# Four graph-attention layers on one core: earlier mask gathers, and two jobs of layer 2 moved to other engines

## The chip, the core and the metric

The kernel runs on one core of one Trainium2 chip. A core has a matmul engine (TensorE), three engines for elementwise work (VectorE, ScalarE, GpSimd), and a queue that issues direct transfers (SyncE). They run side by side and meet at semaphores. The metric is the device time of one execution in microseconds (us). Lower is better.

## The reference

The input is a matrix `x` of 4096 nodes by 256 features and a 0/1 adjacency of 4096 by 4096, which is sparse for most nodes: its density falls with the node's number. Four attention layers follow one another. Each normalizes the rows, applies a relu, projects, and lets every target node average its neighbours with softmax weights; the result is added to `x`.

```python
h = jnp.maximum(_layernorm(x), 0.0)
h = h @ W                                  # layer 2: four heads of 64 columns
e = leaky_relu((h @ a1)[:, None] + (h @ a2)[None, :], 0.2)
attention = softmax(where(adj > 0, e, -inf), axis=1)
x = x + f(attention @ h)                   # f: identity in layers 0 and 2, elu in layer 1
```

Layer 3 has a positive and a negative attention, projects their results together and ends in an elu. Layers 0 and 1 have one head, layer 2 has four, layer 3 counts as two.

## The kernel before, in words

**Tiles and lists.** The 4096 nodes are 32 tiles of 128; four tiles are a block, so there are eight blocks. Targets in the first blocks (`DENSE = (4, 2, 1, 1)` of them in layers 0 to 3) are computed densely: all 32 source tiles are multiplied against the whole block of 512 targets. Later target tiles are computed from a list: four fixed source tiles (`DP`), whose masks are in `mpre`, and then `CAPS[T]` more steps, each of which takes 128 source rows picked by an index. `CAPS` falls from 12 in tile 4 to 6 in tile 31.

**The lists.** `list_sources` works out in layer 0, block by block, which sources a tile needs. Its last step writes `idx_T`, a table of row numbers with one column for each step. Lists for blocks 4 to 7 come up in layer 0 between dense blocks, since those targets are listed there already; those of blocks 1, 2 and 3 follow as the dense blocks' masks are read.

**The gathers.** A listed step needs two indirect DMAs, both issued by GpSimd. `s_gg` (L1189) fetches 128 rows of the layer's table of projected nodes, once for each layer. `mlist` (L895) fetches the mask columns that belong to them; it is fetched once, kept on chip, and used by all later layers. There are 715 of the first kind and 218 of the second. `masks_of` is the queue of mask gathers still to be issued. `gather_masks(n)` issues up to `n` of them after a step of the plan, in the queue's order; `gather_masks(CAPS[T], T)` fetches what tile `T` still lacks at the moment it is needed. The queue's order before is blocks 4 to 7, then 2 and 3, then 1.

**A step of the plan.** `run` walks through a hand-made plan of steps. Each step passes four stages: fetch (gathers are issued), begin (ScalarE, layer 2 only), weigh (VectorE) and multiply (TensorE), at leads of 0, 2, 3 and 6 steps (`LEAD`). After each multiplied step it advances a clock by the unit's `cost` and works off three queues at the unit's `rates`: `posts` (ends of tiles and rows for the next layer), `lists_q`, and the mask gathers. GpSimd executes in exactly the order in which its instructions are written; the order on the other engines is decided by a scheduler.

**Weights in layer 2.** A weight is max(grow, g) times the mask. VectorE does this with one pass for a head (L999). For `nact` of the four heads ScalarE begins instead: relu(grow * g - 1) (L985), and one VectorE pass over these heads together adds 1 and multiplies by the mask (L1008). `nact` is 2 before.

**The end of a tile in layer 2.** `end2` is a generator in `posts`. ScalarE copies the accumulator to `o`, TensorE transposes it, VectorE divides by the sums into `y` and adds `y` to `x` (L1132). A `yield t` lets the plan's clock go on by `t` before the next part is written. `node_rows` of layer 3 starts on a pair of tiles when both are marked in `stored`; its first instruction is the statistics of `x` on VectorE (L672), and its last stores the projected rows to the table. No listed step of a layer can gather before all rows of its table are stored.

**Order of tiles.** In layer 2 the plan begins with 36 dense steps. Tiles 8 to 31 follow and then 4 to 7. The rest of the dense steps is spread between the first 14 tiles. Layer 1 begins with 16 dense steps and has 48 more, two after each listed tile.

Of the kernel before, what the change touches and what calls it, by code (L numbers as in the profile page):

```python
# [20 lines left out]
NT = N // P  # L21
IB = 512
NIB = N // IB
IT = IB // P
# [429 lines left out]
DP = CH  # L454
JT = NT - DP
TS0 = IT
DENSE = (4, 2, 1, 1)
# [3 lines left out]
CAPS = (25, 17, 15, 13, 12, 11, 11, 10, 10, 9, 9, 9, 8, 8, 8, 8) + (8,) + (7,) * 7 + (6,) * 8  # L461
# [11 lines left out]
def list_layers(ctx: ExitStack, tc: tile.TileContext, a: dict, out: bass.AP, flag):  # L473

    nc = tc.nc
# [31 lines left out]
    x = keep.tile([P, NT, D], F32, name="x")  # L507
# [134 lines left out]
    def pump(queue, n, width=1, force=False):  # L642

        k = 0
        while n and k < min(width, len(queue)):
            if queue[k][1] > clock[0] and not force:
                k += 1
                continue
            n -= 1
            try:  # L650
                queue[k][1] = clock[0] + (next(queue[k][0]) or 0.0)
            except StopIteration:
                queue.pop(k)

    def ensure(done):
        while not done():
            assert posts
            pump(posts, 1, force=True)
# [139 lines left out]
    def list_sources(ib, seen, pool, consts):  # L798
# [81 lines left out]
    index = {}  # L880

    masks_of = [
        (T, k)
        for b0, b1 in ((DENSE[0], NIB), (DENSE[1], DENSE[0]), (1, DENSE[1]))
        for T in range(b0 * IT, b1 * IT)
        for k in range(CAPS[T])
    ]
# [1 line left out]
    def gather_masks(n, tile=None):  # L889

        for T, k in list(masks_of):
            if not n or tile is None and T not in index:
                break
            if tile in (None, T):
                nc.gpsimd.indirect_dma_start(  # L895
                    out=mlist[:, OFFS[T] + k, :],
                    out_offset=None,
                    in_=mask_t[T // IT],
                    in_offset=bass.IndirectOffsetOnAxis(ap=index[T][:, k : k + 1], axis=0),
                    element_offset=T % IT * P,  # L900
                )
                masks_of.remove((T, k))
                n -= 1
# [207 lines left out]
    def end2(u, it, T):  # L1111
        big = layers[2].big
        o = big.tile([DH + 1, HEADS, P], F32, name=f"s_o_{T}", tag="o", bufs=2)
        if u.nt == 1:
            nc.scalar.copy(o, u.accs[0])
        else:
            for h in range(HEADS):
                nc.scalar.copy(o[:, h, :], u.accs[h][:, it * P : (it + 1) * P])
        yield 1.0
        tp = ps_mm.tile([P, HEADS, DH + 1], F32, name=f"s_oT_{T}", tag="mm")  # L1120
        for h in range(HEADS):
            nc.tensor.transpose(
                tp[:, h, :], o[:, h, :], ident[0 : DH + 1, 0 : DH + 1]
            )
        yield 3.0
        rz = small.tile([P, HEADS], F32, name=f"s_rz_2_{T}", tag="rz4")
        nc.vector.reciprocal(rz, tp[:, :, DH])
        y = big.tile([P, HEADS, DH], F32, name=f"s_y2_{T}", tag="y2", bufs=2)
        nc.vector.tensor_tensor(
            y, tp[:, :, 0:DH], rz.unsqueeze(2).to_broadcast([P, HEADS, DH]), op=ALU.mult  # L1130
        )
        nc.vector.tensor_add(x[:, T, :], x[:, T, :], y.rearrange("p h o -> p (h o)"))  # L1132
        stored[T] = 2

    firsts = {}
# [39 lines left out]
    def listed_sources(L, T, pool):  # L1175
        heads = list(range(L.H))

        def get(i):
            if i < DP:
                g = L.g[:, i, :] if L.l == 0 else L.pre[:, i, :]  # L1180
                m = mpre[:, i, T * P : (T + 1) * P]
            else:
                ensure(lambda: all(L.ready))
                while T not in index:
                    pump(lists_q, 1, force=True)
                gather_masks(CAPS[T], T)
                k = i - DP
                g = pool.tile([P, GW[L.l]], F32, name=f"s_gg_{L.l}_{T}_{k}", tag="gg")
                nc.gpsimd.indirect_dma_start(  # L1189
                    out=g,  # L1190
                    out_offset=None,
                    in_=L.table,
                    in_offset=bass.IndirectOffsetOnAxis(ap=index[T][:, k : k + 1], axis=0),
                )
                m = mlist[:, OFFS[T] + k, :]
            return heads, [g[:, h * L.part : (h + 1) * L.part] for h in heads], m

        return get

    with ExitStack() as phase:  # L1200
# [28 lines left out]
        L0 = weights(0, prep, prep, nc.scalar)  # L1229
# [80 lines left out]
        def block(ib):  # L1310
            masks = {}

            def get(jt):
                if jt % CH == 0:
                    masks[jt // CH] = mask_chunk(ib, jt // CH)
                for k, at in enumerate(sides):
                    if at == ib * NT + jt:
                        mask_chunk(DENSE[0] + k // NCH, k % NCH)
                ensure(lambda: L0.ready[jt])
                return [0], [L0.g[:, jt, :]], masks[jt // CH][:, jt % CH, :]  # L1320

            return Unit(L0, ib * IT, IT, NT, get, big="growb", rates=(2, 2, 1))

        load_x(0)
        load()
# [9 lines left out]
        for ib in range(DENSE[0]):  # L1335
            for step in block(ib).plan():
                plan.append(step)
                if ib * NT + step[1] >= LISTED0:
                    n = 1 + step[1] % 2
# [10 lines left out]
    gat = ctx.enter_context(tc.tile_pool(name="s_gather", bufs=9))  # L1350
    stream = ctx.enter_context(tc.tile_pool(name="s_stream", bufs=3))
    for l in (2, 3):
        L = weights(l, late, late, nc.sync)
# [11 lines left out]
    for l in (1, 2, 3):  # L1365
        L = layers[l]

        def all_sources(L, T0, nt, heads, per):


            held = {}
            n = L.part
            cols = slice(heads[0] * n, (heads[-1] + 1) * n)
            w = slice(T0 * P, (T0 + nt) * P)

            def get(i):
                jt, k = divmod(i, per)
                jt = ORDER[L.l][jt // CH] * CH + jt % CH
                mine = heads[k : k + 1] if per > 1 else heads
                if jt < DP:  # L1380
                    ensure(lambda: L.ready[jt])
                    return mine, [L.pre[:, jt, h * n : (h + 1) * n] for h in mine], mpre[:, jt, w]
                if jt % CH == 0 and k == 0:
                    ensure(lambda: all(L.ready[jt : jt + CH]))
                    gt = stream.tile(
                        [P, CH, n * len(heads)], F32, name=f"s_gs_{L.l}_{T0}_{jt}_{heads[0]}", tag="gs"
                    )
                    nc.sync.dma_start(gt, table_rows(L.table, jt)[:, :, cols])
                    mt = stream.tile([P, CH, nt * P], U8, name=f"s_ms_{L.l}_{T0}_{jt}_{heads[0]}", tag="ms")
                    nc.sync.dma_start(mt, table_rows(mask_t[T0 // IT], jt)[:, :, 0 : nt * P])  # L1390
                    held["t"] = gt, mt
                gt, mt = held["t"]
                h0 = heads[0]
                return (
                    mine,
                    [gt[:, jt % CH, (h - h0) * n : (h - h0 + 1) * n] for h in mine],
                    mt[:, jt % CH, :],
                )

            return get  # L1400


        if l == 3:
            one = Unit(L, 0, IT, NT, all_sources(L, 0, IT, [0], 1), big="growb", heads=[0])
            two = Unit(L, 0, IT, NT, all_sources(L, 0, IT, [1], 1), big="growb", heads=[1], like=one)
            first = one.plan() + two.plan()
        else:
            per = L.H
            first = []
            for ib in range(DENSE[l]):  # L1410
                first += Unit(
                    L,
                    ib * IT,
                    IT,
                    NT * per,
                    all_sources(L, ib * IT, IT, list(range(L.H)), per),
                    big="o" if ib else "growb",
                    cost=0.9 if l == 2 else 1.7,
                    per=per,
                    rates=(2, 0, 1),  # L1420
                ).plan()
        tiles = []
        tail = DENSE[0] if l == 1 else DENSE[1]
        for T in (*range(tail * IT, NT), *range(DENSE[l] * IT, tail * IT)):
            u = Unit(
                L, T, 1, DP + CAPS[T], listed_sources(L, T, gat), cost=(0, 0.9, 1.2, 0.9)[l], nact=(0, 0, 2, 0)[l]
            )
            tiles.append(u.plan())


        alone, over_tiles = ((0, 0), (16, 24), (36, 14), (16, 28))[l]
        plan += first[:alone]
        rest = first[alone:]
        for k, t in enumerate(tiles):
            plan += t
            n1, n2 = (len(rest) * min(j, over_tiles) // over_tiles for j in (k, k + 1))
            plan += rest[n1:n2]
# [60 lines left out]
```

## Time and profile before

| | before |
|---|---|
| time, median of 3 runs | 1764.71 us (1761.51 to 1771.69) |
| span of the profiled run | 1771.9 us |
| TensorE busy | 1670.8 us (94%), 9268 instructions |
| VectorE busy | 1331.1 us (75%) |
| GpSimd busy | 1068.4 us (60%), 1043 instructions |
| ScalarE busy | 610.2 us (34%) |
| table gathers, L1189 | 715, 1042 ns on the mean |
| mask gathers, L895 | 218, 1105 ns on the mean |
| last table gather of layer 0 issued | 509.7 us |
| last attention matmul of layer 1 ends | 847.0 us |
| first attention matmul of layer 3 | 1352.8 us |

The shares are means over four layers with different limits, so they don't tell what a stage waits for. In the profile's rows PE is TensorE, PEld its weight loads, DVE VectorE, ACT ScalarE, POOL GpSimd and SP SyncE. A row of a group ends with the idle time of its engine before these instructions and with what ended it. Issue time of a DMA isn't counted as busy.

### The profile page before, as it was taken

Reading aid. Unit: us, or ns where it says so; the run is one execution under the profiler, and the core shown is the slowest. Engines: PE = TensorE matmul, PEld = TensorE weight load, DVE = VectorE, ACT = ScalarE, POOL = GpSimd, SP = SyncE. Lnnn points to the kernel's source line nnn. Section 1 sums busy time; section 2 is a strip of 40 time slices with the busy share of each in tenths; the row PEclk is TensorE's granted clock in tenths of the full one; section 3 lists DMA queues with packets and bytes.
Section 4 is the critical chain, followed back from the end, with each engine's and each line's share of the span. In section 5 each row is a group of like instructions: output and inputs, shape, how many; then the busy total and the mean of one; then the engine's idle time right before and its main releaser. Section 6 shows DMA issues by size and latency. Waiting matters only on the chain.

```text
span 1771.9 us, 29224 instructions
## 1 busy us (share of the span) xinstructions
PE 1670.8 (94%) x9268; PEld 1386.0 (78%) x9268; DVE 1331.1 (75%) x3908; ACT 610.2 (34%) x1802; POOL 1068.4 (60%) x1043
## 2 busy tenths in 40 slices
PE   6989999989999899897989999999999999999997
PEld 4877777768878778675467887889998888888886
DVE  6778898878764676654869988998886577777765
ACT  5531011011030132111357767699984011111101
POOL 9665655736566777777775444455571655555563
PEclk9998798989989999998999999999999999999999
DMA  8889767935264444443233333233332666656554
GB/s 270 275 268 296 221 208 230 333 103 184 53 167 138 119 130 136 119 130 88 66 75 97 85 104 86 80 105 104 91 101 74 206 201 181 181 168 183 168 171 125
DMA packets 134530, 271.08 MB, mean 153 GB/s; under 512 B 23186, under 2 KB 52288, under 8 KB 134368
## 3 DMA queue, kind: packets, MB, share of 16 engines
q0 software_dynamic: 48272, 127.55, 27.3%
q1 hardware_dynamic: 85260, 141.04, 24.0%
q8 instruction: 77, 1.26, 0.3%
q14 instruction: 85, 0.70, 0.1%
q10 hardware_dynamic: 836, 0.53, 0.1%
HBM read 228.91 MB, written 40.12 MB: 152 GB/s over the span
## 4 chain that ended last, share of the span: by engine, by line
PE 72%; DVE 10%; DMA 9%; POOL 4%; issue 3%; ACT 2%; SPq 0%; DVEq 0%; ACTq 0%; POOLq 0%
PE s_acc L1035 43%; PE s_accm L1060 17%; PE s_pj L727 6%; DMA s_gg<-table,idx 5%; DVE s_p L999 3%; DMA s_raw<-in_adjT 3%; PE idx_ps L866 2%; POOL mlist L895 2%; PE s_sT L933 1%; PE s_tp L695 1%; DVE first L857 1%; DVE s_m L1277 1%; POOL s_gg L1189 1%; ACT s_p L985 1%; DVE s_p L1008 1%
## 5 line engine op out<-in xcount | busy, mean ns | idle before, releaser
L1189 POOL DMA_INDIRECT s_gg<-table,idx x715 | 745.0, 1042 | 581.8 <-PE s_acc L1035 239.1
L999 DVE SCALAR_TENSOR_TENSOR s_p<-s_grow,s_gg,mlist 128x128 f32<-128x128 f32 x1151 | 367.8, 346 | 195.3 <-DMA s_gg<-table,idx 124.6
L1035 PE MATMUL s_acc<-s_gg,s_p 128*128 128x257 f32 x1430 | 358.1, 391 | 28.0 <-DVE s_p L999 27.7
L1035 PEld LDWEIGHTS s_acc<-s_gg,s_p 128*128 128x128 f32 x1430 | 267.5, 193 | 84.0 <-DVE s_p L999 48.4
L1035 PE MATMUL s_acc<-g,s_p 128*128 128x257 f32 x1152 | 298.3, 404 | 5.0 <-DVE s_p L999 5.0
L895 POOL DMA_INDIRECT mlist<-mask_t,idx x218 | 240.9, 1105 | 76.0 <-issue 56.4
L1035 PEld LDWEIGHTS s_acc<-g,s_p 128*128 128x128 f32 x1152 | 226.4, 202 | 38.2 <-DVE s_p L999 6.7
L999 DVE SCALAR_TENSOR_TENSOR s_p<-s_grow,pre,mpre 128x128 f32<-128x128 f32 (+1 forms) x576 | 190.3, 369 | 39.7 <-PE s_acc L1035 31.2
L1035 PE MATMUL s_acc<-s_gs,s_p 128*128 128x257 f32 x896 | 217.1, 398 | 0.0
L1060 PE MATMUL s_accm<-s_p,s_gg 128*65 128x128 f32 x1744 | 207.2, 274 | 3.4 <-DVE s_p L1008 2.7
L1035 PEld LDWEIGHTS s_acc<-s_gs,s_p 128*128 128x128 f32 x896 | 178.0, 200 | 32.0 <-DVE s_p L999 4.9
L1060 PEld LDWEIGHTS s_accm<-s_p,s_gg 128*65 128x65 f32 x1744 | 193.9, 138 | 8.6 <-DVE s_p L1008 5.1
L985 ACT ACTIVATE s_p<-s_grow,s_minus,s_gg 128x128 f32<-128x128 f32 x436 | 186.7, 486 | 36.8 <-DMA s_gg<-table,idx 23.1
L999 DVE SCALAR_TENSOR_TENSOR s_p<-s_grow,s_gs,s_ms 128x512 f32<-128x512 f32 x224 | 162.4, 749 | 45.0 <-PE s_accm L1060 21.0
L1035 PE MATMUL s_acc<-pre,s_p 128*128 128x257 f32 x768 | 181.8, 381 | 0.3 <-ACT s_y L1146 0.2
L727 PE MATMUL s_pj<-s_w,s_hT 128*128 128x259 f32 (+3 forms) x640 | 165.4, 399 | 7.7 <-ACT s_hT L697 3.7
L939 ACT ACTIVATE s_grow<-s_sT 128x256 f32<-128x256 f32 (+2 forms) x136 | 46.8, 367 | 341.8 <-PE s_sT L933 332.8
L1035 PEld LDWEIGHTS s_acc<-pre,s_p 128*128 128x128 f32 x768 | 143.4, 191 | 21.8 <-ACT s_y L1146 0.6
L727 PEld LDWEIGHTS s_pj<-s_w,s_hT 128*128 128x128 f32 x640 | 121.8, 197 | 31.5 <-ACT s_hT L697 6.4
L1060 PE MATMUL s_accm<-s_p,pre 128*65 128x128 f32 (+1 forms) x928 | 120.3, 284 | 4.8 <-DVE s_p L1008 4.8
L1060 PEld LDWEIGHTS s_accm<-s_p,pre 128*65 128x65 f32 x928 | 103.9, 138 | 21.6 <-issue 14.6
L985 ACT ACTIVATE s_p<-s_grow,s_minus,pre 128x128 f32<-128x128 f32 x224 | 96.3, 487 | 19.1 <-issue 11.9
(123 smaller groups left out, 1658.1 us busy)
## 6 DMA issues: line engine op xcount, KB each, us to landing
s_raw<-in_adjT SPq DMA_DIRECT2D x128, 512.0 KB
s_gs<-table SPq DMA_DIRECT2D x28, 516.0 KB
mask_t<-s_m SPq DMA_DIRECT2D x56, 256.0 KB
s_gg<-table,idx POOLq DMA_INDIRECT x715, 3.5
s_ms<-mask_t SPq DMA_DIRECT2D x35, 256.0 KB
table<-s_g SPq DMA_DIRECT2D x28, 258.0 KB
table<-g SPq DMA_DIRECT2D x8, 516.0 KB
x<-in_x SPq DMA_DIRECT2D x8, 512.0 KB
```

Of the source, the lines that this page charges most:

```text
L695: nc.tensor.transpose(tp[:, c, :], zs[k][:, c * P : (c + 1) * P], ident)
L727: nc.tensor.matmul(ps, lhsT=hT[:, c, :], rhs=L.w[:, c, k * (D + 6) : k * (D + 6) + cols], start=(c == 0), stop=(c == 1),)
L857: nc.vector.tensor_tensor(first, place, lof[:, t, j : j + half].unsqueeze(1).to_broadcast([P, P, half]), op=ALU.is_equal,)
L866: nc.tensor.matmul(ps[:, 0:cap], lhsT=first[:, :, j % half], rhs=val[:, 0:cap, j * IT + t], start=(j == 0), stop=(j == JT - 1),)
L895: nc.gpsimd.indirect_dma_start(out=mlist[:, OFFS[T] + k, :], out_offset=None, in_=mask_t[T // IT], in_offset=bass.IndirectOffsetOnAxis(ap= ...
L933: nc.tensor.transpose(ps[:, h - h0, it, :], L.s[:, T0 + it, h : h + 1].to_broadcast([P, P]), ident)
L939: nc.scalar.activation(grow[:, h1:h2, :], ps[:, h1 - h0 : h2 - h0].rearrange("p h a b -> p h (a b)"), AF.Exp, scale=scale,)
L985: nc.scalar.activation(w[:, h, :], u.grow[:, h, :], AF.Relu, scale=g[h][:, n - 1 : n], bias=minus)
L999: nc.vector.scalar_tensor_tensor(p[:, k, :], u.grow[:, h, :], g[k][:, n - 1 : n], m, op0=ALU.min if L.l == 3 and h == 1 else ALU.max, op1= ...
L1035: nc.tensor.matmul(u.accs[it][h], lhsT=p[:, k, it * P : (it + 1) * P], rhs=g[k][:, 0:n], start=first, stop=last,)
L1060: nc.tensor.matmul(u.regions[h], lhsT=g[k][:, 0 : DH + 1], rhs=p[:, k, :],  start=first and (u.nt > 1 or h == 0), stop=last, skip_group_ch ...
L1189: nc.gpsimd.indirect_dma_start(out=g, out_offset=None, in_=L.table, in_offset=bass.IndirectOffsetOnAxis(ap=index[T][:, k : k + 1], axis=0),)
```

## The change

Three parts. First, the queue of mask gathers takes blocks 1, 2 and 3 in their own order after blocks 4 to 7; an entry whose list isn't ready is passed over where it stopped the walk before; dense steps of layer 0 issue two mask gathers in place of one, and the dense steps of layer 2 issue none. It is for having the masks in before layers 1 and 2 need GpSimd for table gathers. Second, the addition to `x` at the end of a tile in layer 2 goes from VectorE to GpSimd, 2.0 on the plan's clock after `y`. Third, in tiles 6, 9, ..., 30 of layer 2 ScalarE begins three heads and VectorE does one by itself. Parts two and three are for relieving VectorE.

```diff
-        for b0, b1 in ((DENSE[0], NIB), (DENSE[1], DENSE[0]), (1, DENSE[1]))
+        for b0, b1 in ((DENSE[0], NIB), (1, DENSE[0]))
...
         for T, k in list(masks_of):
-            if not n or tile is None and T not in index:
-                break
-            if tile in (None, T):
+            if n and T in index and tile in (None, T):
                 nc.gpsimd.indirect_dma_start(
...
-        nc.vector.tensor_add(x[:, T, :], x[:, T, :], y.rearrange("p h o -> p (h o)"))
+        yield 2.0
+        nc.gpsimd.tensor_add(x[:, T, :], x[:, T, :], y.rearrange("p h o -> p (h o)"))
         stored[T] = 2
...
-            return Unit(L0, ib * IT, IT, NT, get, big="growb", rates=(2, 2, 1))
+            return Unit(L0, ib * IT, IT, NT, get, big="growb", rates=(2, 2, 2))
...
-                    rates=(2, 0, 1),
+                    rates=(2, 0, 1 if l == 1 else 0),
...
-                L, T, 1, DP + CAPS[T], listed_sources(L, T, gat), cost=(0, 0.9, 1.2, 0.9)[l], nact=(0, 0, 2, 0)[l]
+                L, T, 1, DP + CAPS[T], listed_sources(L, T, gat), cost=(0, 0.9, 1.2, 0.9)[l], nact=(0, 0, 3 if T % 3 == 0 else 2, 0)[l]
```

## The prediction

> **What bounds the kernel now.** I read the page's slices first, then the table of windows with boundaries at the layers' first and last matmuls, then GpSimd's timeline, then the chain. The slices say that TensorE is busy nearly everywhere, but a busy TensorE is modelled, so I looked for stretches where it waits.
>
> ```profile
> PE   6989999989999899897989999999999999999997
> POOL 9665655736566777777775444455571655555563
> PEclk9998798989989999998999999999999999999999
> ```
>
> The windows (PE, PEld, DVE, ACT, POOL busy with counts, then clock and DMA):
>
> ```profile
> 138.00:511.00 373.00, 349.41 (x1983) 292.08 (x1984) 305.06 (x781) 52.45 (x192) 218.79 (x193) 0.89 0.63 197
> 557.00:846.00 289.00, 261.27 (x1101) 205.59 (x1101) 174.18 (x544) 61.40 (x213) 220.83 (x224) 0.93 0.44 120
> 947.00:1157.00 210.00, 210.00 (x1409) 161.60 (x1407) 186.83 (x556) 145.67 (x373) 98.81 (x89) 1.00 0.33 88
> 1157.00:1353.00 196.00, 191.46 (x1610) 183.18 (x1609) 170.90 (x613) 177.36 (x498) 105.97 (x98) 1.00 0.35 97
> ```
>
> The reader is to see layer 1 (557 to 846): GpSimd is busy 221 of 289 us, which looks loose. Its timeline tightens it, because every gather is followed by 0.30 us of issue:
>
> ```profile
> 837.02 0.95 POOL L895 DMA_INDIRECT mlist<-mask_t,idx  x1 [0.30 <-issue]
> 838.28 0.94 POOL L895 DMA_INDIRECT mlist<-mask_t,idx  x1 [0.30 <-issue]
> ...
> 889.39 0.94 POOL L1189 DMA_INDIRECT s_gg<-table,idx  x1 [0.30 <-DMA mlist<-mask_t,idx]
> ```
>
> 224 x 0.30 = 67 us more, 288 of 289: GpSimd is full, and layer 1 is bound by its gathers. The lines from 837 to 889 are 36 mask gathers in a row at the turn to layer 2, ahead of layer 2's first table gather. The chain agrees (window 815 to 945):
>
> ```profile
> by line: POOL mlist L895 28.4%; DMA s_gg<-table,idx 14.8%; issue 12.6%; PE s_accm L1060 11.1%; DVE s_p L999 7.5%; DMA mlist<-mask_t,idx 5.8%; POOL s_gg L1189 5.1%; PE s_acc L1035 4.3%; DVE s_p L1008 3.0%; ACT s_p L985 2.9%; PE s_pj L727 0.7
> ```
>
> In layer 0 the chain runs over TensorE, loads of the adjacency and VectorE; GpSimd idles 95 us there (gaps over 0.31 us, 145 to 511, summed from the timeline). In layer 2 from 947 to 1157 the chain is TensorE alone; from 1157 to 1353 TensorE, VectorE and ScalarE are all near full. Layer 3 is TensorE's.
>
> **What the Trainium skill says.** "GPSIMD Engine Reference", Elementwise side-by-side cycle accounting: a two-input add takes about twice as long on GpSimd. The trace agrees: 128x256 adds take 861 ns on GpSimd (L685), 421 on VectorE (L1132). The same page, Key points: GpSimd shares SBUF interfaces with VectorE. The trace fits: a gather takes 0.94 us at least, but 218.79/193 = 1.13 on the mean in layer 0, 0.99 in layer 1 where VectorE is less busy. "TensorE: Matmul & The Clock Gate", What's actually happening: a window of little work halves TensorE's clock. The trace agrees: 0.66 in 890 to 900, after a wait. "DMA: Bandwidth & Descriptors", Anatomy of one DMA: about 2 us of fixed latency per gather; here a table gather lands 2.7 to 7.2 us after issue (median 3.5).
>
> **Part 1, mask gathers.** 218 remain; they move. From the order of GpSimd's instructions in both programs: before, layer 0 holds 105 mask and 105 table gathers; after, blocks 1 and 2 and 5 gathers of tile 12 join them, 44 + 37 + 5 = 86. Between layer 0's and layer 1's table gathers stand 14 masks in both. Layer 1's own stretch then has 174 table and 13 mask gathers, none from tile 23 on. The 36 at the turn and those inside layer 2's first tiles are gone.
>
> *Layer 0.* GpSimd works in order, and a mask gather waits for its tile's list. The lists come from VectorE, whose order here is unchanged: tile 20's is written at 189.2. After the change the gathers for tile 20 stand right behind tile 16's eight table gathers, so GpSimd waits there until 189.3 and has 296 - 29 - 8 = 259 gathers to go. At layer 0's pace (1.13 + 0.30 = 1.43) that is 370 us: the last is issued near 560, against 510 before. Behind these masks in the queue stand the table gathers of tiles 17 to 31; their multiplies (TensorE, then VectorE's weights) wait. I compared issue plus 4.5 us with the time of each multiply before: up to tile 20 they arrive within about 5 us, tile 22's are 16 late, tile 28's about 40. So layer 0 ends about 49 us later. At 1.25 (the uncontended pace) it would be 2, at 1.50 (more contention) 68; I take 1.43, since VectorE has the same work to do beside it.
>
> *Layer 1.* First table gather 22 us after layer 0's last, as before (509.7 to 531.9; the 14 masks take 18): 582. Then 187 x (0.99 + 0.30) = 240, plus 6 for the wait for buffers at the start (6.4 at 554): last gather 828. Before, the last matmul came 10 us after the last gather: 838. TensorE alone (each f32 matmul leaves two records; spacings from the chain): between 557 and 846 there are 901 attention records, so 450 matmuls, at 0.434 (64 records in 13.89 us) = 195, projections 23, transposes and rows 10: 228 us; 557 + 49 + 228 = 834. The two nearly meet. Layer 1 ends near 838 against 847: -9.
>
> *Turn to layer 2.* From 885 to 947 TensorE spends 62 us on 144 listed matmuls at 0.218 (24 records in 2.62 us), 13.5 dense ones at 0.86 (20 records in 8.75 us) and 5.4 us of projections and transposes, 48 us in all; the rest is waiting behind the masks, partly at half clock. With the queue free when the table is ready I count 10 of the 14 us: -10.
>
> **Part 2, the add on GpSimd.** Removed: 32 x 0.42 = 13.5 us of VectorE. Added: 32 x (0.86 + 0.30) = 37 us of GpSimd, and a wait: GpSimd's add waits for y, and behind it stand the next table gathers. Laying y's times in before against the gathers that follow each add in the new order, tiles 9 to 21 stop GpSimd for 5 to 10 us each. Those gathers were issued 7 to 10 us early, and TensorE still has 1.5 us or more in hand: hidden by the queue of weighted tiles. In tiles 4 to 7, where GpSimd is full (13 gathers in 20 us from 1280), each add costs about 1 us. VectorE's order also changes: the statistics of the new x come 0.7 to 4.8 us of VectorE work after y (9 us before for half of the tiles), and now wait for GpSimd's 1.3 us: some 0.6 us in about half of the tiles, on an engine that is not the bound until 1157. I take +4, between 0 and +12. At the end of layer 2 the table gather of layer 3 was issued at 1377, used at 1388: room for the add and the delay of 2.0.
>
> **Part 3, three heads on ScalarE.** Tiles 6, 9, ... 30: 68 listed + 36 fixed steps = 104. Each adds an activation (487 ns by itself; 8 take 3.09 us in the chain, so 0.39 apart) and widens one VectorE pass from 256 to 384 instead of a pass of 128. ScalarE gets 41 us, VectorE loses some 0.13 x 104 = 14. Up to 1157 TensorE covers both. After it, 45 such steps (tiles 24, 27, 30 and 6) add 17 us to a ScalarE that has 19 us left (177 of 196). VectorE's relief offsets the crowding: 0, between -5 and +15.
>
> Sum: 49 - 58 (layer 1's shortening) - 10 + 4 + 0 = -15: 1764.7 - 15 = 1750.
>
> **Rivals.** (A) Layer 0 absorbs the masks better: its 95 us idle speak for it, the lists' dates against it. At a pace of 1.33 layer 0 ends 24 us late (189.3 + 259 x 1.33 = 534), layer 1 at 189.3 + 344 + 22 + 240 + 16 = 812 or, by TensorE, 557 + 24 + 228 = 809: -35 - 10 + 4 = -41: 1724. (B) It ends slower: the pace falls to 1.50 with more DMAs beside the adjacency loads, and TensorE at half clock. Then 578 + 22 + 187 x 1.33 + 16 = 865, +18; the turn returns 8, layer 2 costs 8: 1783. For it: 300 to 340, where 26 gathers ran unbroken, went at 1.54. Against: 440 to 460 at 1.33. (C) The masks give -19, but layer 2 takes it: ScalarE at 0.487 a step needs 22 us where 19 are left, and VectorE waits for GpSimd's adds: +19 in all, so 1765. For it is that stretch's three nearly full engines, against it ScalarE's spacing of 0.39.
>
> **Chances.** Forecast 0.42, A 0.18, B 0.20, C 0.20. Faster takes A and most of the forecast (0.37): 0.55; same, the rest of the forecast and most of C: 0.22; slower, B and the tail of C: 0.23. The range 1725 to 1782 reaches from A's time to B's.
>
> **What would show it.** Right: the last table gather of layer 0 near 560 instead of 510, with unbroken 0.30 gaps before it; layer 1's last near 828 and few waits of VectorE on gathers after tile 22; no mask gathers after about 690; layer 2's first table gather at once when its table lands; GpSimd waits of 5 to 10 us on VectorE's y up to 1150 with TensorE full. Wrong: a layer 0 that ends by 530 (A) or after 575 (B), TensorE waiting on ScalarE in layer 2's tail (C), or mask gathers whose mean is far from 1.1 us.

## The result and the profile after

The changed kernel takes 1817.05 us (median of 4 runs, 1814.05 to 1828.65) against 1768.20 for the kernel before beside it (1761.51 to 1772.34): a ratio of 1.0295, 95% interval 1.0245 to 1.0346, so 49 us slower. The forecast of 1750 was wrong in its sign, and the time lies outside its range.

In the kernel after, lines from L895 on carry a number two lower, and from the add in `end2` on one lower: the mask gather is L893, the write of `y` L1127, GpSimd's add L1131, the table gather L1188. The slices of its page, in tenths:

```profile
PE   6988878779888999999999999999999999999997
POOL 8756565775777677567254454555564465555463
PEclk9989798987988999999999999999999999999999
```

From the third slice to the thirteenth (91 to 594 us) TensorE shows 7 and 8 in all but one, where before it showed 9 in all but two. The windows, cut again at the layers' borders (columns as before):

```profile
163.00:596.00 433.00, 354.20 (x1870) 281.39 (x1869) 285.02 (x736) 45.47 (x165) 290.23 (x268) 0.87 0.52 156
643.00:890.00 247.00, 239.17 (x1102) 199.04 (x1101) 172.23 (x542) 61.46 (x213) 170.33 (x173) 0.99 0.49 137
970.00:1200.00 230.00, 225.08 (x1497) 173.62 (x1496) 195.76 (x537) 172.43 (x454) 112.51 (x106) 0.99 0.31 87
1200.00:1406.00 206.00, 192.63 (x1565) 182.04 (x1563) 165.54 (x525) 185.00 (x525) 117.01 (x115) 0.98 0.33 90
```

Layer 1 is 42 us shorter (247 against 289) and now TensorE's: 239 of 247 busy, GpSimd down from 221 to 170. The turn is clean: in GpSimd's timeline the last table gather of layer 1 and the first of layer 2 follow one another, with no mask between them:

```profile
880.71 0.95 POOL L1188 DMA_INDIRECT s_gg<-table,idx  x1 [0.30 <-PE s_acc L1033]
921.56 0.94 POOL L1188 DMA_INDIRECT s_gg<-table,idx  x1 [39.90 <-PE s_accm L1058]
```

But layer 0 has grown, and layer 2 too. The groups of the page show what new waits there are:

```profile
L997 DVE SCALAR_TENSOR_TENSOR s_p<-s_grow,s_gg,mlist 128x128 f32<-128x128 f32 x1083 | 355.0, 354 | 253.7 <-DMA s_gg<-table,idx 171.3
L893 POOL DMA_INDIRECT mlist<-mask_t,idx x218 | 240.0, 1101 | 141.7 <-DVE idx L876 74.1
L1131 POOL TENSOR_TENSOR x<-x,s_y 128x256 f32<-128x256 f32 x32 | 28.5, 891 | 153.0 <-DVE s_y L1127 152.9
```

The 218 mask gathers take 1101 ns each, as before, but GpSimd stood idle 74 us in front of them for lists (`idx`, L876) that VectorE had not written. VectorE in turn waited 171 us for table gathers (125 before). In front of its 32 adds in layer 2 GpSimd stood idle 153 us for `y`; before, it had no add there and no such wait.

The table follows the issue of table gathers through the kernel (us from the start of each profiled run):

| | before | after | later by |
|---|---|---|---|
| layer 0, last | 509.7 | 595.9 | 86.2 |
| layer 1, last | 835.8 | 880.7 | 44.9 |
| layer 2, first of its second tile (9) | 909.5 | 935.1 | 25.6 |
| layer 2, last | 1345.8 | 1398.5 | 52.7 |
| end of the span | 1771.9 | 1826.5 | 54.6 |

Layer 0 lost 86 us, layer 1 gave back 41, the turn 19; layer 2 lost 27 more; layer 3 took 2 us longer. (The two profiled runs differ by 54.6 us, 6 more than the medians.) Two losses had to be explained: layer 0's, which the forecast had as 49, and layer 2's, which it had as 4.

### The profile page after: what moved, and what is told of

Same layout as the page of the kernel before. It is cut to its first block, busy times and chain, and to the rows that moved or that the text cites. A ratio compares the mean times of both kernels' runs of the same rounds, so it can differ in the third digit from the quotient of the medians.

```text
span 1826.5 us, 29042 instructions
## 1 busy us (share of the span) xinstructions
PE 1685.0 (92%) x9268; PEld 1393.5 (76%) x9268; DVE 1326.2 (73%) x3772; ACT 643.1 (35%) x1906; POOL 1085.0 (59%) x1075
## 4 chain that ended last, share of the span: by engine, by line
PE 65%; DMA 10%; POOL 7%; DVE 6%; issue 6%; ACT 5%; SPq 0%; DVEq 0%; POOLq 0%; ACTq 0%
PE s_acc L1033 38%; PE s_accm L1058 17%; DMA s_gg<-table,idx 6%; PE s_pj L727 6%; POOL mlist L893 4%; ACT s_p L983 3%; DVE s_p L997 2%; POOL s_gg L1188 2%; DMA mlist<-mask_t,idx 2%; PE idx_ps L866 2%; PE s_sT L931 1%; PE s_tp L695 1%; DMA s_raw<-in_adjT 1%; POOL s_z L681 1%; DVE first L857 1%
## 5 line engine op out<-in xcount | busy, mean ns | idle before, releaser
L1188 POOL DMA_INDIRECT s_gg<-table,idx x715 | 735.0, 1028 | 401.7 <-PE s_acc L1033 198.1
L997 DVE SCALAR_TENSOR_TENSOR s_p<-s_grow,s_gg,mlist 128x128 f32<-128x128 f32 x1083 | 355.0, 354 | 253.7 <-DMA s_gg<-table,idx 171.3
L893 POOL DMA_INDIRECT mlist<-mask_t,idx x218 | 240.0, 1101 | 141.7 <-DVE idx L876 74.1
L1033 PE MATMUL s_acc<-g,s_p 128*128 128x257 f32 x1152 | 315.2, 421 | 8.4 <-DVE s_p L997 8.2
L1033 PEld LDWEIGHTS s_acc<-g,s_p 128*128 128x128 f32 x1152 | 234.7, 211 | 50.4 <-DVE s_p L997 16.5
L983 ACT ACTIVATE s_p<-s_grow,s_minus,s_gg 128x128 f32<-128x128 f32 x504 | 212.4, 485 | 36.4 <-PE s_accm L1058 17.2
L997 DVE SCALAR_TENSOR_TENSOR s_p<-s_grow,pre,mpre 128x128 f32<-128x128 f32 (+1 forms) x540 | 182.5, 373 | 46.1 <-PE s_acc L1033 33.2
L1033 PE MATMUL s_acc<-s_gs,s_p 128*128 128x257 f32 x896 | 206.9, 384 | 0.0
L1033 PEld LDWEIGHTS s_acc<-s_gs,s_p 128*128 128x128 f32 x896 | 170.7, 192 | 28.1 <-DVE s_p L997 4.0
L727 PE MATMUL s_pj<-s_w,s_hT 128*128 128x259 f32 (+3 forms) x640 | 173.5, 414 | 13.3 <-ACT s_hT L697 7.7
L1131 POOL TENSOR_TENSOR x<-x,s_y 128x256 f32<-128x256 f32 x32 | 28.5, 891 | 153.0 <-DVE s_y L1127 152.9
```

The costliest lines, as they stand in the source:

```text
L727: nc.tensor.matmul(ps, lhsT=hT[:, c, :], rhs=L.w[:, c, k * (D + 6) : k * (D + 6) + cols], start=(c == 0), stop=(c == 1),)
L893: nc.gpsimd.indirect_dma_start(out=mlist[:, OFFS[T] + k, :], out_offset=None, in_=mask_t[T // IT], in_offset=bass.IndirectOffsetOnAxis(ap= ...
L983: nc.scalar.activation(w[:, h, :], u.grow[:, h, :], AF.Relu, scale=g[h][:, n - 1 : n], bias=minus)
L997: nc.vector.scalar_tensor_tensor(p[:, k, :], u.grow[:, h, :], g[k][:, n - 1 : n], m, op0=ALU.min if L.l == 3 and h == 1 else ALU.max, op1= ...
L1033: nc.tensor.matmul(u.accs[it][h], lhsT=p[:, k, it * P : (it + 1) * P], rhs=g[k][:, 0:n], start=first, stop=last,)
L1131: nc.gpsimd.tensor_add(x[:, T, :], x[:, T, :], y.rearrange("p h o -> p (h o)"))
```

## Experiments

The sessions differed: in those of e1 to e8 and of e17 and e18 the kernel before took 1947 to 1951 us, in the others 1765 to 1768, with layers 0 to 2 longer and layer 3 much as here (436 against 426 us in e1, from layer 2's last table gather to the end). It wasn't the chip alone, since one chip showed both levels. So every ratio is against the kernel before in the same session, and times of a stage are compared only within a level. Stage times come from one profiled run each, so some us of them are chance. Layers 0 and 1 of e2, e5, e6, e7 and e17 are those of the kernel before, so they serve as its stages at the longer level. The profiled run of e18 took 32 us more than its median, so its stages are left out.

| run | what | ratio to before, 95% interval | layer 0's last table gather | layer 2, tile 9's first to last table gather |
|---|---|---|---|---|
| longer level | as before | 1 | 527 to 554 (five runs) | |
| e1 | part 1 alone | 1.0109 (1.0079 to 1.0138) | 659.0 | 466 |
| e2 | parts 2 and 3 | 1.0157 (1.0082 to 1.0233) | 527.5 | 503 |
| e3 | part 1, masks 25 us after lists, 3 a step | 1.0030 (1.0005 to 1.0055) | 649.1 | 469 |
| e4 | part 1 with the old order rule | 1.0207 (1.0143 to 1.0271) | 612.6 | 475 |
| e5 | part 2 alone | 1.0168 (1.0091 to 1.0244) | 553.8 | 500 |
| e6 | part 3 alone | 1.0044 (1.0007 to 1.0082) | 535.3 | 477 |
| e7 | masks off the turn | 0.9928 (0.9902 to 0.9954) | 540.1 | 510 |
| e8 | part 1, ten buffers | 1.0208 (1.0125 to 1.0291) | 700.9 | 467 |
| e17 | the add's wait without its work | 1.0199 (1.0127 to 1.0272) | 545.3 | 500 |
| e18 | the add's work without its wait | 1.0047 (1.0024 to 1.0071) | | |
| shorter level | as before | 1 | 493 to 510 (five runs) | 436 |
| e9 | layer 0's masks behind their lists, none added | 1.0283 (1.0257 to 1.0309) | 552.2 | 437 |
| e10 | masks off the turn, spread | 0.9922 (0.9897 to 0.9947) | 504.5 | 440 |
| e11 | part 2, delay 12.0 | 1.0184 (1.0154 to 1.0214) | 507.4 | 434 |
| e12 | part 2's delay alone | 1.0006 (0.9988 to 1.0024) | 493.1 | 434 |
| e13 | part 1, masks 25 us after lists, 2 a step | 0.9941 (0.9924 to 0.9957) | 527.2 | 440 |
| e14 | part 2, delay 12.0, not the last tiles | 1.0083 (1.0050 to 1.0115) | 503.8 | 432 |
| e15 | the version put together | 0.9803 (0.9763 to 0.9844) | 507.9 | 440 |
| e16 | part 1 alone again | 1.0186 (1.0150 to 1.0223) | 588.4 | 441 |

### Which part

e1 (and later e16) is the change without GpSimd's add (L1131) and the third head:

> Part 1 alone (the gathers of masks moved), with the add on VectorE and two heads on ScalarE throughout. Changed kernel minus old: +49 us. Theory 1 (GpSimd waits in order for lists that VectorE has not written, VectorE waits for table gathers behind them, and layer 2 loses by itself because of parts 2 and 3): layer 0's last table gather issued near 596 us, layer 1's last near 881, layer 2 then takes no longer than before, so about +24 us against the kernel before (near 1792). Rival (layer 2's loss is a consequence of the moved masks, for example of a late start): near +49 (1817).

> Part 1 alone, the same kernel as the first run, for the stages beside e13 on one chip. Layer 0's last table gather near +86, layer 1's last near +45, layer 2 no longer than before from its tile 9 on: +20 to +30 us in all. Rival: +49, if layer 2's loss came with the masks.

Measured: +22 us at the longer level, +33 at the shorter, and layer 2 then takes 441 us from tile 9 on, against 436. So layer 2's loss doesn't come with the masks. e2 is the complement:

> Parts 2 and 3 alone, masks as before. Theory 1: layers 0 and 1 as before (last table gather of layer 0 near 510), and layer 2 loses 25 us by itself: near 1793. Prediction's costs (+4 and 0): near 1772. Rival (the loss of layer 2 comes with the moved masks): no change, 1768.

Measured: +29 us in the median (1976.24 against 1947.39), layer 2 at 503 us against e1's 466. It is the second and third part that cost layer 2. Each alone:

> Part 2 alone: GpSimd adds the results to x in layer 2, 2.0 of plan time later; two heads on ScalarE throughout, masks as before. Theory 2 (the add makes VectorE's statistics and GpSimd's next gathers wait, and layer 2 pays): 15 to 30 us slower than before, all of it in layer 2. Rival (the third head on ScalarE is what costs): within 8 us of before. The prediction's term was +4.

> Part 3 alone: three heads on ScalarE in every third tile of layer 2, the add on VectorE as before, masks as before. Theory 2: within 8 us of before, or faster by up to 5, since VectorE loses 14 us of work. Rival (ScalarE is the bound from tile 24 on): 10 to 30 us slower, with the loss in the last 200 us of layer 2. The prediction's term was 0.

The add alone: layer 2 at 500, +32 us. The three heads alone: layer 2 at 477 (466 to 475 in the four runs with neither), the run about 9 us slower by its ratio, at the edge of "within 8". The add is the larger loss by far. At the level of the result parts 2 and 3 were not run without part 1. There the whole change is 16 us slower than e16 (49 against 33 over before), and its layer 2 takes 23 us more (463 against 441).

### Layer 0: count, lists or buffers

e3 holds a mask gather back until its list must long be there. Against part 1 (lines of rates shortened, here and below):

```diff
+            listed_at[T] = clock[0]
...
-            if n and T in index and tile in (None, T):
+            if n and T in index and tile in (None, T) and (tile == T or clock[0] - listed_at[T] >= 25.0):
...
-  rates=(2, 2, 2)
+  rates=(2, 2, 3)
```

> Part 1 alone, but a mask gather is issued only 25 us of plan time after its list was planned, at up to 3 a step: 186 mask gathers in layer 0 against 191 in part 1 alone and 105 before. Theory 1 (waiting for lists): waits of GpSimd on lists fall from about 74 us to under 15, layer 0's last table gather is issued at 560 or earlier, and the run is 30 to 40 us shorter than part 1 alone. Rival (the number of gathers at 1.43 us each fills layer 0): last table gather within 8 us of part 1 alone's, run within 8 us of it.

The waits on lists fell to 2 us, yet layer 0 ended only 10 us sooner than in e1's profiled run, which was itself 19 us below e1's median. By medians e3 is 15 us shorter than e1, where theory 1 had 30 to 40: a miss. GpSimd's idle time had moved to the table gathers, which waited 107 us for buffers. The timelines show what three a step does; first GpSimd, then VectorE:

```profile
253.73 0.94 POOL L895 DMA_INDIRECT mlist<-mask_t,idx  x1 [0.30 <-issue]
254.97 0.94 POOL L895 DMA_INDIRECT mlist<-mask_t,idx  x1 [0.30 <-issue]
256.22 0.95 POOL L1189 DMA_INDIRECT s_gg<-table,idx  x1 [0.30 <-issue]
```

```profile
247.87 0.26 DVE L829 TENSOR_TENSOR pos<-pos,sums 128x112 f32<-128x112 f32 x1
260.30 0.35 DVE L999 SCALAR_TENSOR_TENSOR s_p<-s_grow,s_gg,mlist 128x128 f32<-128x128 f32 x1 [12.17 <-remote]
```

Twelve mask gathers in a row, from 241 on, stand before one table gather; VectorE stands still for 12.17 us, until 4 us after that gather's issue. ("remote" is a releaser that the trace doesn't resolve; a gather's landing fits it.)

e4 keeps the old `break` at the first tile without a list, with two mask gathers a step:

> Part 1 alone, but with the old rule that a tile without a list holds up all behind it: blocks 1 and 2 begin only after tile 31's masks, 137 mask gathers in layer 0. Theory 1: waits on lists little more than before (10 us), lists as early as before, last table gather of layer 0 between 515 and 556; total between -25 and +10 us against before. Rival (number of gathers): 32 more gathers at 1.43 give +46 in layer 0, and with 67 masks left in layer 1 the run is at least 10 us slower than before.

A miss: only 32 more masks than before in layer 0, but 83 us of waits on lists, and a layer 0 of 613. The backlog, and not the `break`, had kept the masks of the old kernel behind their lists: at two a step there is none.

e8 gives GpSimd more buffers to run ahead with:

```diff
-  name="s_gather0", bufs=7
+  name="s_gather0", bufs=10
```

> Part 1 alone with ten buffers for layer 0's table gathers in place of seven; all else as in the run of part 1 alone. Theory 3 (with seven buffers GpSimd can run only about seven gathers ahead, so its idle time between two bursts of masks can't be used and a burst stands in front of the next table gather): last table gather of layer 0 at least 25 us earlier than with seven, run 20 us or more shorter than part 1 alone. Rival A (GpSimd waits for lists that VectorE writes late): no change within 8 us, since a deeper ring brings no list sooner. Rival B (the count of gathers at the pace they go): no change within 8 us.

Theory 3 fell: layer 0 ended at 701, against 659 in e1. The waits for buffers went down (25 to 11 us), those on lists up (110 to 171). That fits a GpSimd that, free to run further ahead, meets the missing list earlier; why layer 0 also got longer isn't shown.

e9 separates count from place. It adds no gather anywhere, and only lets each stand right behind its list:

```diff
-  rates=(2, 2, 1)
+  rates=(2, 2, 2)
...
-            if not n or tile is None and T not in index:
+            if not n or tile is None and (T not in index or T < low):
...
-                gather_masks(u.rates[2])
+                gather_masks(u.rates[2], low=0 if u.L.l else DENSE[0] * IT)
```

> The kernel before with up to two mask gathers a step in layer 0 instead of one, and only those of tiles 16 to 31: 105 mask gathers in layer 0 as before, and all other layers as before, but each gather now stands right behind its list. Theory 1 (waits on lists): GpSimd waits 50 us or more on lists in layer 0, last table gather of layer 0 at least 40 us later than before, run 30 us or more slower, though no gather was added. Rival (the number of gathers): layer 0 within 10 us of before, run within 8 us. In between, both share the loss of part 1.

Measured: +49 us, as much as the whole change, with 105 mask gathers in layer 0 as before; its last table gather came 42 us later than in the profile of before. And e13 separates them from the other side: more gathers, no waits (e3's delay, two a step):

> Part 1 alone, with mask gathers only 25 us of plan time after their list and at most two a step: 169 mask gathers in layer 0, 64 more than before and 22 fewer than part 1 alone. Theory A (waits on lists make up half of part 1's +86): waits on lists under 15 us, last table gather of layer 0 between +10 and +50 against before. Theory B (each added gather costs its full 1.3 us in layer 0, wherever it stands, since GpSimd's idle time lies in other stretches): +70 to +100 with hardly a wait on lists, the idle time now at the buffers.

Measured: 64 gathers more than before, layer 0 only 17 us longer than in the profile of before, and the run 10.8 us faster than before, 44 faster than e16 in the same session. The waits from 125 to 620 us, of before, after, e9 and e13 in turn (us in total, times, longest):

```profile
POOL s_gg L1189 <- PE s_acc L1035: 101.2, 56, 15.4
...
POOL mlist L895 <- DVE idx L876: 6.4, 2, 5.6
...
DVE s_p L999 <- DMA s_gg<-table,idx: 19.0, 19, 1.8
```

```profile
POOL mlist L893 <- DVE idx L876: 66.8, 7, 21.3
...
POOL s_gg L1188 <- PE s_acc L1033: 5.5, 18, 0.3
...
DVE s_p L997 <- DMA s_gg<-table,idx: 103.8, 46, 5.6
```

```profile
POOL s_gg L1189 <- PE s_acc L1035: 89.6, 43, 20.7
POOL mlist L895 <- DVE idx L876: 73.8, 4, 27.9
...
DVE s_p L999 <- DMA s_gg<-table,idx: 65.5, 34, 4.2
```

```profile
POOL s_gg L1189 <- PE s_acc L1035: 48.0, 33, 20.2
...
DVE s_p L999 <- DMA s_gg<-table,idx: 50.2, 29, 6.1
```

Before, GpSimd's idle time was at table gathers that waited for a free buffer (101 us): it was ahead, and hardly anybody waited for it. After, that slack is gone (5.5 us), 67 us went into lists, and VectorE waits 104 us for gathers. e9 shows the list waits with the slack still there (90): idle time in other stretches doesn't pay for them. In e13 the added gathers took half of the slack (48 left), there is no line for lists, and VectorE's waits are half of after's. The window takes in the start of layer 1 where layer 0 is shorter. Up to layer 0's own last table gather VectorE's waits are 2 us before, 103 after, 61 in e9 and 39 in e13, so the readings stand.

### Layer 2: the add

e12 keeps the add on VectorE, 2.0 of plan time later; e11 has it on GpSimd 12.0 later, e14 the same for tiles 8 to 31 alone:

> The delay of part 2 alone: the add to x stays on VectorE but comes 2.0 of plan time later. Theory 2: within 5 us of before, since no gather waits for it. Rival (the later emission of the add, with the statistics right behind it, costs layer 2): 15 us slower or more.

> Part 2 alone, with 12.0 of plan time before GpSimd's add in place of 2.0. Theory 2 (GpSimd, which runs ahead of VectorE, stands still at the add until y is there, and the table gathers behind it come late): waits of GpSimd on y under 30 us in layer 2 against 108 us, the loss of 33 us in layer 2 gone, run within 8 us of before (the last tiles may start layer 3 some us late). Rival (VectorE waits for GpSimd's slower add before its statistics, or the two share a port): loss stays within 8 us of the run with 2.0.

> Part 2 with 12.0 of plan time before GpSimd's add, for tiles 8 to 31 alone; tiles 4 to 7 and the dense block keep the add on VectorE, at once. Theory 2 with the turn (the add costs layer 2 only through GpSimd standing still at it, and the 31 us of the run with 12.0 everywhere arose after layer 2's last gather, since the last tiles' x came late): within 6 us of before. Rival (GpSimd's adds cost VectorE or TensorE in layer 2 in another way): 15 us slower or more.

The delay of 2.0 alone costs nothing (1.0006). With 12.0 layer 2 lost nothing between tile 9 and its end, though GpSimd still waited 47 us on `y` there (under 30 were expected): not every wait costs. But the runs were 31 and 15 us slower: the time came back after layer 2's last gather (456 us to the end in e11, 443 in e14, 426 before). The work that waits with the add is layer 3's rows: in the 77 us after layer 2's last matmul TensorE still had projections to do, 48 records of matmuls in e11 and 32 in e14, 16 before. So the expectation of e14, that the last tiles alone did this, missed; and since the delay also moves work, these two don't isolate the wait. e17 and e18 do. e17 adds on VectorE, and lets GpSimd only touch y at that place; e18 has GpSimd add as much of something that is ready. The first added line is in both, the second in e17, the third in e18 (the lines that make `touch` and `idle` are left out):

```diff
+        yield 2.0
         nc.vector.tensor_add(x[:, T, :], x[:, T, :], y.rearrange("p h o -> p (h o)"))
...
+        nc.gpsimd.tensor_add(touch, y[:, 0, 0:4], y[:, 0, 4:8])
...
+        nc.gpsimd.tensor_add(idle, idle, idle)
```

> The add to x on VectorE, 2.0 of plan time later (a delay that cost nothing by itself), and at that place GpSimd reads only eight numbers a row of y: it waits for y as the add did, with next to no work. Theory 2 (standing still at y makes the table gathers behind it late): 15 to 30 us slower than before, with 80 us or more of waits of GpSimd on y in layer 2. Rival (GpSimd's slower add, and what waits for its result, is what costs): within 6 us of before.

> The add to x on VectorE, 2.0 of plan time later, and at that place GpSimd adds two other 128x256 operands that depend on nothing: the same work in the same place of its queue, without the wait. Theory 2 (the wait is what costs): within 6 us of before. Rival (GpSimd's time, or its sharing of SBUF with VectorE, is what costs): 15 us slower or more.

The wait without the work: +36 us, more than the 15 to 30 expected, and layer 2 at 500, as with the whole add (e5). The work without the wait: +8 us (5 to 14 by the interval of its ratio), a little over the 6 of theory 2. Of e17, the largest wait of the window 1050 to 1560 (us in total, times, longest), and one of its times in GpSimd's timeline:

```profile
POOL s_touch L1135 <- DVE s_y L1129: 175.3, 27, 11.4
```

```profile
1103.42 0.31 POOL L1135 TENSOR_TENSOR s_touch<-s_y 128x4 f32<-128x4 f32 x1 [10.41 <-DVE s_y L1129]
1104.13 1.57 POOL L1192 DMA_INDIRECT s_gg<-table,idx  x1 [0.40 <-ACT s_p L985]
```

GpSimd stood still for 10.41 us before an instruction of 0.31, and the table gathers behind it started after it. The Trainium skill ("GPSIMD Engine Reference", Key points) says that GpSimd shares its SBUF interfaces with VectorE; whatever that costs, e18 has it, together with GpSimd's own time, in its 8 us for 32 adds. It isn't the main cost.

### The turn, and a faster version

e7 and e10 take block 1's 36 masks off the turn and gather them within layer 2, in tiles 12 to 15 (e7) or one in about three steps from tile 12 on (e10). The last line is e10's; e7 has a 1 there, for tiles 12 to 21:

```diff
-                    rates=(2, 0, 1),
+                    rates=(2, 0, 1 if l == 1 else 0),
...
+  rates=(2, 0, 0.34 if l == 2 and T >= 12 else 0)
```

> The kernel before with one thing moved: the 36 mask gathers of block 1 that stand at the turn from layer 1 to layer 2 are not gathered in layer 2's dense block; they follow one at a time in layer 2's tiles 12 to 15, where GpSimd is half idle. Layers 0 and 1 hold what they held before. The prediction's term for the turn was -10: near 10 us faster than before if the masks at the turn are what layer 2's first gathers wait for. Rival (the turn waits for the table's rows and the dense block, not for the masks): within 3 us of before. Second rival (the masks cost the same wherever they stand): within 3 us too, but with layer 2's first table gather earlier and tiles 12 to 15 later by as much.

> The kernel before with the 36 mask gathers of block 1 taken from the turn to layer 2 and gathered one in about three steps in layer 2's tiles 12 to 23. The run that put them into tiles 12 to 15 was 14 us faster than before. If a burst is what costs there (tiles 12 to 15 were some 40 us slower), spreading gives another 10 to 20 us: 25 to 35 faster than before. Rival (each mask gather costs layer 2 the same wherever it stands): 10 to 18 us faster, as in the other run.

Both gain: 0.9928 and 0.9922. e7's first gather of layer 2 came 46 us after layer 1's last, where e6 with the masks there took 89; but from tile 9's first table gather to tile 15's it took 147 us (107 in e6), and most of the gain went back. Spread, the masks cost layer 2 only 4 us (440 against 436), yet the gain is the same 14 us, not the 25 to 35 expected. That is the number of the rival (the same cost wherever the masks stand), but not for its reason: at this level the turn had less to give. From layer 1's last table gather to the first of tile 9 it takes 55 us in e10 and 74 before (61 in e7 and 113 in e6).

e15 puts together what worked: e10's turn, and in layer 0 up to three masks in two steps, each at least 15 us of plan time after its list, tiles 8 to 15 where none of tiles 16 to 31 is due:

> The spread turn (14 us faster than before) and in layer 0 three mask gathers in two steps, each at least 15 us of plan time after its list, tiles 8 to 15 wherever tiles 16 to 31 have none ready: 125 in layer 0 against 105, 49 in layer 1 against 71, and block 1's all in layer 2. If evenly spread gathers fit into layer 0's idle time: last table gather of layer 0 within 8 us of before, layer 1 some 26 us shorter (20 x 1.3), run 30 to 45 us faster than before. If each costs its full 1.3 us: layer 0 +26, layer 1 -26, run as the spread turn alone, 10 to 18 faster than before.

Measured: 1731.52 us against 1765.36, 34 us faster than before, where the change was 49 slower. 20 masks more in layer 0 and it ends at 507.9, among the 493 to 510 of before; layer 1 is 25 us shorter. Its slices:

```profile
PE   6988999889989999999999999999989999999997
POOL 8755874756766777775266666555661665554563
```

## Why the prediction was wrong

The stages add up: layer 0 was off by +37 us, layer 1 by +17, the turn by -9 and layer 2 by +23. That is 68 of the 70 us between the forecast of -15 and the 54.6 of the profiled runs.

*Layer 0, forecast +49, measured +86: the step that failed.* The step said "The lists come from VectorE, whose order here is unchanged: tile 20's is written at 189.2", and let 259 gathers follow that one wait without another. The count was right, and the pace was good: from 196.6 to 597 there are 400 us, of which 42 went into five further waits on lists, so 358 / 259 = 1.38 each where 1.43 was taken (12 us less). The 42 us had been put at nothing, and tile 20's list came at 196.2, 7 later: 7 + 42 - 12 = 37, and 49 + 37 = 86. The 7 us are chance: in e16, whose layer 0 is the same, this list came at 189.5 and layer 0's last table gather at 588.4, again with 44 us of further waits on lists. Unchanged order doesn't mean unchanged dates: VectorE reaches a list only after the weights ahead of it, and those wait for table gathers that stand in GpSimd's queue behind masks that wait for lists. GpSimd's and VectorE's timelines show one turn of this loop in the kernel after:

```profile
196.58 1.54 POOL L893 DMA_INDIRECT mlist<-mask_t,idx  x1 [21.35 <-DVE idx L876]
...
248.74 1.32 POOL L1188 DMA_INDIRECT s_gg<-table,idx  x1 [0.30 <-PE s_sT L931]
...
264.85 1.54 POOL L893 DMA_INDIRECT mlist<-mask_t,idx  x1 [11.04 <-DVE idx L876]
```

```profile
254.54 0.35 DVE L997 SCALAR_TENSOR_TENSOR s_p<-s_grow,s_gg,mlist 128x128 f32<-128x128 f32 x1 [4.78 <-DMA s_gg<-table,idx]
...
264.41 0.17 DVE L876 TENSOR_SCALAR idx<-idx_ps 128x12 int32<-128x12 f32 x1 [1.45 <-PE idx_ps L866]
```

After the wait for tile 20's list GpSimd issues one gather after another, but the table gathers, with the masks between them, are late now. VectorE waits for eight of them before it writes the list of tile 4 (the only one with 12 columns), 18 us in all; before, it waited for none in this stretch. From the one list to the other it takes 68 us where it took 51, and GpSimd stands still for tile 4's list again. The last list of all came at 576.7, 88 us later than before.

e9 shows that the place alone costs 42 to 59 us (against the five layers 0 of before at its level), e13 that gathers which don't wait for lists cost less than their own time: 17 to 34 us for 64, against 88 at 1.38 each. What isn't settled is e3, where gathers without list waits cost nearly as much as with them (109 us against 119 in e1, from the mean of the five at that level). It differs from e13 in three a step instead of two, in 17 more gathers, and in the level of its session; the burst above is a sign of the first, not a proof.

*Layer 1, forecast -58, measured -41: right in kind, too large.* 44 gathers fewer brought 0.94 us each, not 1.3. In e13 and e15, with 22 fewer, the stretch between the last table gathers of layers 0 and 1 shrank by 27 and 25 us (326 to 299 and 301), 1.2 each: so the price holds until TensorE takes over, and TensorE's own time had been put too low (228; it was busy 239 in a stretch of 247).

*Turn, forecast -10, measured -19* (from layer 1's last table gather to tile 9's first). e10, which changes nothing but the place of these masks, shortens it by as much and gains 14 us in all: the mechanism was right.

*Part 2, forecast +4: the second step that failed.* The stops of 5 to 10 us were foreseen, and called "hidden by the queue of weighted tiles". e17 puts the wait alone at 36 us (at the longer level) and e18 the work alone at 8. The loss is where the stops are: from tile 9's first table gather to tile 16's it takes 137 us after and 123 in e16, and VectorE and ScalarE wait 23 us for table gathers in layer 2 where they wait 7 in e16. That TensorE had 1.5 us in hand was read from the kernel before, gather by gather; what a reserve seen there is worth against 27 waits of up to 11.4 us (e17) was not asked.

*Part 3, forecast 0 (-5 to +15), measured about +9 alone (e6):* within its bounds, on the bad side. Rival C's reason, a ScalarE without room, fits: VectorE waits 22 us for ScalarE's part of the weights in layer 2 after, 9 in e16. No run isolates that reason, and the term is a small part of the whole.

*The rivals.* B, the only slower one, gave 1783 by a slower pace of the gathers. Its sign came true, a layer 0 that ends after 575, but not its reason: the pace was in fact better. C had VectorE wait for GpSimd's adds; it was GpSimd that waited for VectorE's `y`. None of the cases had a wait that feeds on itself.

## What to carry to other kernels

Idle time of an in-order engine is room for more work only if that work never waits there: before moving an instruction into such a queue, ask when its operand is written and whether that date depends on what now stands behind it. Keep a distance between the producer and the in-order consumer (here 15 to 25 us of plan time); what had looked like a needless backlog was that distance. It isn't enough by itself: e3 kept it and still lost with three gathers a step, while e13 with two and e15 with three in two steps gained. In a queue of gathers the wait of a foreign instruction can cost more than its work: here 0.31 us of touching `y` cost as much as the whole add.

## Not expected of the hardware

The same kernel took 1765 to 1768 us in some sessions and 1947 to 1951 in others, on one chip both; the longer level has its time in layers 0 to 2, hardly in layer 3, which gathers too (436 us in e1 against 426). The granted clock of the kernel before is 0.92 to 0.94 there and 0.96 to 0.97 here; whether that is cause or effect, and what differs, wasn't found. GpSimd's indirect gathers kept their 0.94 us plus 0.30 us of issue at both levels.
